# Two attention blocks on one core: four of a Strassen group's seven products add up in one PSUM bank

## The chip, the cores and the metric

The kernel runs on 1 core of one Trainium2 chip. The metric is device time in microseconds (us). Before the change it is 3025.81 us, the median of 3 runs (3024.51 to 3025.86). The engines are TensorE (PE; PEld is its weight load), VectorE (DVE), ScalarE (ACT), GpSimd (POOL) and SyncE (SP, which issues the DMAs).

## The reference, cut to what matters

x is 8 images of 512 channels by 1024 positions, in fp32. Two attention blocks follow each other, each with a residual.

```python
# block 0: group norm over 32 groups, 8 heads of 64 channels
h = group_norm(x, norm_w, norm_b)
q, k, v = split(qkv_w @ h + qkv_b)
attn = softmax(q^T k / sqrt(64))          # per head
x = x + proj_w @ (attn v) + proj_b
# block 1: norm over the whole image, one head of 512 channels
n = norm(x) * gn_gamma + gn_beta
q, k, v = wq @ n + bq, wk @ n + bk, wv @ n + bv
attn = softmax(q k^T * 512**-0.5)
x = x + wo @ (attn v) + bo
```

## The kernel before

The core works through the 8 images one after the other; everything is fp32, in tiles of 128 partitions by 512 columns. Weights of block 1 are multiplied together once (wq with wk, wv with wo), so that block 1 has a q, a v, scores and a weighted sum, and no k and no projection of its own.

All products of 512 channels by 1024 positions are split in quarters and done by Strassen's scheme in its Winograd form: 7 products of quarters instead of 8, with sums S1 to S4 of the one side's quarters (`finish`, L171) and T1 to T4 of the other's (`Combined`, L336). Output quarter (0,0) is P1+P2; U2 is P1+P6, U3 is U2+P7, U4 is U2+P5; then (0,1) is U4+P3, (1,0) is U3+P4 and (1,1) is U3+P5.

One group of seven products for a 128-by-512 piece of each output quarter is the generator `strassen` (L362). It is called with `multiply`, which puts a product into a PSUM bank (`by_channels` L422, `by_positions` L434 and local ones for the scores, L743, and the weighted sum, L805), and with `done`, which takes a finished output quarter to SBUF (L452, L466, L683, L750, L811). A product is two matmuls of 512 columns, or four of 256, and four matmuls in the weighted sum; in the profile each fp32 matmul is two rows. A group yields five times, and what the caller hangs on those steps (`at_steps`, hooks) is put between the steps: norms of the next image, sums T, loads.

PSUM is one pool with two tags, o and s, of two buffers each (`banks`, L90). A tile has two banks. A group before the change takes four of them: o for P1 and P2, s for P5 and P6, o for P7 and P4, s (or o) for P3. ACT copies P1 to SBUF as u1; VectorE makes u2, u4 and u3 with `plus` (L373), reading one bank and one SBUF tile each, and the four `done` passes. The u tiles come from a pool of five buffers (L83).

Engine orders of PE, ACT and DVE are those of the program text (`manual_schedule`, L836); a tile framework adds semaphores between engines. The order of an image is: v of block 0 (2 groups), q and k of chunks 1 and 3 of the four channel chunks (2), attention of 8 heads (no Strassen), the projection (2 groups in turn, `together`, L404, with the last divide as a hook, L694), q and k of chunks 0 and 2 for the next image (2, with block 1's norm in hooks, L868), q of block 1 (2), v (2), scores (4), and the weighted sum, called values here (2 groups in turn, with the sums S and T by `finish_values`, L781, in hooks 1, 3 and 5, and the next image's load, norm and T in `at_values`, L883). That is 18 groups per image, 4 of them in pairs that take turns. Hook n runs after step n of the stage. `sums` (L797) is called by the first `done` of the values stage and puts two reciprocals on VectorE.

The lines named by the steps of the prediction are: L427 and L441 (matmuls of q, k, p and of v), L745 (scores), L807 (values), L380 (ACT's copy u1), L375 (`plus`), L454, L468, L752, L817 (first passes of `done`), L326 and L328 (the two halves of a norm, ACT and DVE), L529 and L534 (`held` on ACT and the reciprocal on DVE), L793 (T of the values stage).

Of the kernel before, what the change touches and what calls it, by code (L numbers as in the profile page):

```python
# [59 lines left out]
def two_attention_blocks(  # L60
# [212 lines left out]
    class Norm:  # L273
# [45 lines left out]

        def normed(self, hs):  # L320
            for half in range(2):
                for cc in range(NC):
                    h, x = piece(hs, cc, half), piece(self.xs, cc, half)
                    scale, shift = self.scale[:, cc : cc + 1], self.shift[:, cc : cc + 1]
                    if cc % 2:
                        nc.scalar.activation(h, x, AF.Identity, bias=shift, scale=scale)  # L326
                    else:
                        nc.vector.tensor_scalar(h, x, scale, shift, ALU.mult, ALU.add)  # L328
# [32 lines left out]

    def strassen(multiply, done, name, last="s"):  # L362

        def two(tag, n, *parts):
            o = banks(tag, f"ps_{name}_{n}")
            for i, (a, b) in enumerate(parts):
                multiply(o[:, i, :], a, b)  # L370
            return o[:, 0, :], o[:, 1, :]

        def plus(bank, u, what):  # L373
            t = tile_u(f"{what}_{name}")
            nc.vector.tensor_tensor(t, bank, u, ALU.add)  # L375
            return t

        p1, p2 = two("o", 0, ("A11", "B11"), ("A12", "B21"))
        u1 = tile_u(f"u1_{name}")
        nc.scalar.copy(u1, p1)  # L380
        done(0, 0, p2, u1)
        yield
        o = banks("s", f"ps_{name}_1")
        p5, p6 = o[:, 0, :], o[:, 1, :]
        multiply(p5, "S1", "T1")
        yield
        multiply(p6, "S2", "T2")
        u2 = plus(p6, u1, "u2")
        u4 = plus(p5, u2, "u4")
        yield  # L390
        p7, p4 = two("o", 2, ("S3", "T3"), ("A22", "T4"))
        u3 = plus(p7, u2, "u3")
        done(1, 1, p5, u3)
        done(1, 0, p4, u3)
        yield
        p3, _ = two(last, 3, ("S4", "B22"))
        done(0, 1, p3, u4)
        yield
# [23 lines left out]
    def by_channels(w, c, bs):  # L422


        def multiply(bank, a, b):
            for k in range(2):
                nc.tensor.matmul(  # L427
                    bank, w[a][:, k, c * P : (c + 1) * P], bs[b][:, k, :],
                    start=k == 0, stop=k == 1,
                )  # L430

        return multiply

    def by_positions(w, n2, bs):  # L434


        def multiply(bank, a, b):
            for u in range(2):
                n = 2 * n2 + u
                for k in range(2):  # L440
                    nc.tensor.matmul(  # L441
                        bank[:, u * 2 * P : (u + 1) * 2 * P], bs[b][:, k, n * P : (n + 1) * P],
                        w[a][:, k, :], start=k == 0, stop=k == 1,
                    )

        return multiply

    def make_channels(w, c, oc, bs, bias, to, name, last="s"):

        def done(i, half, bank, u):  # L452
            n = oc + 2 * i
            nc.vector.scalar_tensor_tensor(  # L454
                to(n, half), bank, bias[:, n : n + 1], u, ALU.add, ALU.add
            )

        return strassen(by_channels(w, c, bs), done, f"{name}_{oc}", last)

    def make_v(w, n2, bs, vs, name):  # L460


        def pairs(t):
            return t.rearrange("p (u o) -> p u o", u=2)

        def done(i, half, bank, u):  # L466
            v = vs[2 * half + n2][:, :, i * 2 * P : (i + 1) * 2 * P]
            nc.vector.tensor_tensor(v, pairs(bank), pairs(u), ALU.add)  # L468

        return strassen(by_positions(w, n2, bs), done, f"{name}_{n2}")  # L470
# [72 lines left out]
    def pairs_qk(w, oc, bs, qs, ks, b):  # L543

        for ts, n, bias, name, last in [(qs, 0, V_BQ0, "q", "s"), (ks, 1, V_BK0, "k", "o" if oc else "s")]:
            for i in (oc, oc + 2):
                ts[i] = tile2(f"{name}_0_{b}_{i}")
            yield make_channels(
                w.parts[n], 0, oc, bs, vec[:, bias : bias + NC],
                lambda chunk, half, ts=ts: ts[chunk][:, half, :], f"{name}_0_{b}", last,  # L550
            )
# [3 lines left out]
    def layer0(bs, qs, ks, b, load_next, norm_next):  # L555
# [81 lines left out]
        if norm_next is not None:  # L637
            hooks[0] = [lambda: norm_next().mean_of_all()]
            hooks[2] = [lambda: norm_next().variance_of_all()]
            combine = Combined(f"0_{b + 1}")  # L640
            hooks[3] = [lambda: norm_next().normed(norm_next().xs)]
            hooks[5] = [lambda: combine.first(norm_next().xs)]
# [39 lines left out]
        def project(w, c):  # L682
            def done(i, half, bank, u):  # L683
                chunk = c + 2 * i
                t, x = tile_u(f"p_{b}_{chunk}_{half}"), piece(xs, chunk, half)
                nc.vector.scalar_tensor_tensor(  # L686
                    t, bank, bias[:, chunk : chunk + 1], u, ALU.add, ALU.add
                )
                nc.vector.tensor_tensor(x, x, t, ALU.add)  # L689
                norm.of_half(chunk, half)  # L690
# [15 lines left out]
    def attention1(xs, bs, b, at_values):  # L706
# [35 lines left out]
        def scores(t):  # L742
            def multiply(bank, a, b):  # L743
                for k in range(2):
                    nc.tensor.matmul(  # L745
                        bank, bs[b][:, k, t * P : (t + 1) * P], q_parts[a][:, k, :],
                        start=k == 0, stop=k == 1,
                    )

            def done(i, j, bank, u):  # L750
                p = ps[j][t // 2][i][:, t % 2, :]
                nc.vector.tensor_tensor(p, bank, u, ALU.add)  # L752
                nc.scalar.activation(p, p, AF.Exp, scale=C**-0.5)  # L753
                if late:
# [49 lines left out]
        def values(c):  # L804
            def multiply(bank, a, b):  # L805
                for kt in range(NT // 2):
                    nc.tensor.matmul(  # L807
                        bank, v_parts[kt // 2][a][:, kt % 2, c * P : (c + 1) * P],
                        p_parts[kt // 2][b][:, kt % 2, :], start=kt == 0, stop=kt == NT // 2 - 1,
                    )  # L810

            def done(i, j, bank, u):
                if not invs:
                    sums()
                chunk = c + 2 * i
                t, x = tile_u(f"o_1_{b}_{chunk}_{j}"), piece(xs, chunk, j)
                nc.vector.tensor_tensor(t, bank, u, ALU.add)  # L817
                nc.vector.tensor_tensor(t, t, invs[j], ALU.mult)  # L818
                nc.vector.scalar_tensor_tensor(  # L819
# [16 lines left out]
    with tc.manual_schedule(engines={PE, ACT, DVE}):  # L836
# [15 lines left out]
        for b in range(B):  # L852
            ahead = []

            def load_next():
# [7 lines left out]
            steps = [  # L863
                norm.mean_of_all, norm.variance_of_all, lambda: norm.normed(hs),
                lambda: combine.first(hs), combine.second,
            ]
# [9 lines left out]
            if b + 1 < B:  # L876
# [3 lines left out]
                def load_again():  # L880
                    again.xs = load_x(b + 1, nc.sync)

                at_values = {  # L883
                    2: [load_again], 6: [lambda: again.normed(again.xs)],
                    8: [lambda: combine_next.first(again.xs)], 9: [combine_next.second],
                }
# [409 lines left out]
```

## Time and profile before

| what | value |
|---|---|
| median of 3 runs | 3025.81 us |
| the profiled execution's own time | 3028.86 us |
| its span, first to last instruction | 3027.1 us |
| mean granted TensorE clock | 0.993 |
| attention of block 0, one image (1243.6 to 1360.9 us) | 117.3 us |
| projection (1360.9 to 1388.0) | 27.1 us |
| q and k for the next image, norm beside (1388.0 to 1414.2) | 26.2 us |
| q, v of block 1 (1414.2 to 1462.4) | 48.2 us |
| scores of block 1 (1462.4 to 1510.5) | 48.1 us |
| values of block 1 (1510.5 to 1561.1) | 50.6 us |

The profile is of one execution. Its page gives busy time by engine, the chain of work that ended last, and the costliest groups of instructions. A line of a group reads: line, engine, operation, out<-in with shapes, count, busy time and mean, then the idle time before it and who ended that. In the timeline the first two numbers are start and duration in us, and an idle time with its releaser stands in brackets. Matmuls are pipelined: a row's record is longer than the distance to the next row. The stages in the table are windows of image 3, counted from 0.

### The profile page before, as it was taken

Reading aid. Unit: us, or ns where it says so; the run is one execution under the profiler, and the core shown is the slowest. Engines: PE = TensorE matmul, PEld = TensorE weight load, DVE = VectorE, ACT = ScalarE, POOL = GpSimd, SP = SyncE. Lnnn points to the kernel's source line nnn. Section 1 sums busy time; section 2 is a strip of 40 time slices with the busy share of each in tenths; the row PEclk is TensorE's granted clock in tenths of the full one; section 3 lists DMA queues with packets and bytes.
Section 4 is the critical chain, followed back from the end, with each engine's and each line's share of the span. In section 5 each row is a group of like instructions: output and inputs, shape, how many; then the busy total and the mean of one; then the engine's idle time right before and its main releaser. Section 6 shows DMA issues by size and latency. Waiting matters only on the chain.

```text
span 3027.1 us, 33513 instructions
## 1 busy us (share of the span) xinstructions
PE 2966.2 (98%) x14082; PEld 1379.1 (46%) x14082; DVE 2234.1 (74%) x2746; ACT 899.1 (30%) x1265; POOL 13.9 (0%) x26
## 2 busy tenths in 40 slices
PE   7999999999999999999999999999999999999898
PEld 4533545335453455434553345533545335453353
DVE  4588577884778858787587965889667895668857
ACT  0163122621136111461115501154011640216311
POOL 0000000000000000000000000000000000000000
PEclk9999999999999999999999999999999999999999
DMA  6300213001130112201121020310212102120000
GB/s 238 140 13 25 73 35 125 2 27 71 50 111 1 49 49 83 77 1 49 49 96 65 1 73 25 108 53 1 73 38 95 53 25 73 35 96 3 1 0 29
DMA packets 49935, 167.41 MB, mean 55 GB/s; under 512 B 3440, under 2 KB 9584, under 8 KB 43376
## 3 DMA queue, kind: packets, MB, share of 16 engines
q1 hardware_dynamic: 45824, 160.97, 15.0%
q10 hardware_dynamic: 3952, 4.22, 0.4%
q8 instruction: 112, 1.84, 0.2%
q14 instruction: 47, 0.39, 0.0%
HBM read 137.39 MB, written 27.79 MB: 55 GB/s over the span
## 4 chain that ended last, share of the span: by engine, by line
PE 93%; DVE 6%; issue 0%; ACT 0%; DMA 0%; POOL 0%; POOLq 0%; DVEq 0%
PE s L583 15%; PE ps_o L604 15%; PE ps_q L427 13%; PE ps_v L441 13%; PE ps_s L745 13%; PE ps_o L807 9%; PE ps_k L427 6%; PE ps_p L427 5%; PE ps_sum L618 2%; DVE inv L534 2%; DVE p L686 1%; PE ps_wvo L509 1%; DVE x L819 0%; DVE x L689 0%; DVE o L818 0%; PE ps_sum L800 0%
## 5 line engine op out<-in xcount | busy, mean ns | idle before, releaser
L520 ACT ACTIVATE p<-s 128x1024 f32<-128x1024 f32 x512 | 523.5, 1024 | 333.6 <-PE s L583 329.6
L583 PE MATMUL s<-q,k 64*64 64x512 f32 x4096 | 533.8, 593 | 0.0
L604 PE MATMUL ps_o<-p,v 64*64 64x512 f32 x4096 | 528.7, 589 | 0.0
L522 DVE TENSOR_TENSOR acc<-acc,p 128x1024 f32<-128x1024 f32 x384 | 469.6, 1223 | 76.9 <-ACT p L520 61.9
L534 DVE RECIPROCAL inv<-ps_sum 128x512 f32<-128x512 f32 x80 | 268.4, 3355 | 40.4 <-ACT held_sum L529 40.4
L583 PEld LDWEIGHTS s<-q,k 64*64 64x64 f32 x4096 | 149.6, 133 | 300.6 <-issue 227.8
L604 PEld LDWEIGHTS ps_o<-p,v 64*64 64x64 f32 x4096 | 156.6, 133 | 282.8 <-issue 270.4
L807 PE MATMUL ps_o<-t_p,s_v 128*128 128x512 f32 x384 | 169.7, 595 | 3.6 <-DVE t_p L793 3.6
L745 PE MATMUL ps_s<-s_q,t 128*128 128x512 f32 x384 | 170.0, 592 | 0.0
L753 ACT ACTIVATE p<-p 128x512 f32<-128x512 f32 x128 | 80.1, 630 | 253.0 <-DVE p L752 253.0
L375 DVE TENSOR_TENSOR u_s<-ps_s,u_s 128x512 f32<-128x512 f32 x96 | 66.4, 692 | 117.6 <-PE ps_s L745 116.5
L380 ACT COPY u_v<-ps_v 128x512 f32<-128x512 f32 x32 | 18.7, 585 | 433.4 <-PE ps_v L441 433.4
L380 ACT COPY u_q<-ps_q 128x512 f32<-128x512 f32 x32 | 18.7, 585 | 413.5 <-PE ps_q L427 413.5
L375 DVE TENSOR_TENSOR u_q<-ps_q,u_q 128x512 f32<-128x512 f32 x96 | 66.4, 691 | 96.8 <-PE ps_q L427 95.7
L752 DVE TENSOR_TENSOR p<-ps_s,u_s 128x512 f32<-128x512 f32 x128 | 86.6, 687 | 68.6 <-ACT u_s L380 67.6
L468 DVE TENSOR_TENSOR v<-ps_v,u_v 128x512 f32<-128x512 f32 x128 | 82.7, 683 | 62.8 <-ACT u_v L380 61.7
L807 PEld LDWEIGHTS ps_o<-t_p,s_v 128*128 128x128 f32 x384 | 71.6, 190 | 99.1 <-issue 82.0
L745 PE MATMUL ps_s<-q,h 128*128 128x512 f32 x256 | 115.1, 592 | 0.0
L745 PEld LDWEIGHTS ps_s<-s_q,t 128*128 128x128 f32 x384 | 73.0, 190 | 91.8 <-issue 88.0
L441 PE MATMUL ps_v<-w_wvo,t 128*128 128x256 f32 x512 | 113.1, 379 | 0.0
L427 PE MATMUL ps_q<-t,w_wqk 128*128 128x512 f32 x256 | 112.5, 592 | 0.0
L807 PE MATMUL ps_o<-p,v 128*128 128x512 f32 x256 | 112.5, 592 | 0.0
(179 smaller groups left out, 3862.1 us busy)
## 6 DMA issues: line engine op xcount, KB each, us to landing
x<-in_x SPq DMA_DIRECT2D x88, 512.0 KB, 7.9
w_qk<-stored_qk SPq DMA_DIRECT2D x14, 1792.0 KB, 7.4
out<-x SPq DMA_DIRECT2D x32, 512.0 KB, 2.8
w_wqk<-stored_wqk SPq DMA_DIRECT2D x8, 1792.0 KB, 7.4
w_wvo<-stored_wvo SPq DMA_DIRECT2D x8, 1792.0 KB, 7.5
w_v<-stored_v SPq DMA_DIRECT2D x7, 1792.0 KB, 7.4
w_p<-stored_p SPq DMA_DIRECT2D x7, 1792.0 KB, 7.1
stored_qk<-w_qk SPq DMA_DIRECT2D x2, 1792.0 KB, 7.3
```

What stands on the lines that cost most here:

```text
L375: nc.vector.tensor_tensor(t, bank, u, ALU.add)
L427: nc.tensor.matmul(bank, w[a][:, k, c * P : (c + 1) * P], bs[b][:, k, :], start=k == 0, stop=k == 1,)
L441: nc.tensor.matmul(bank[:, u * 2 * P : (u + 1) * 2 * P], bs[b][:, k, n * P : (n + 1) * P], w[a][:, k, :], start=k == 0, stop=k == 1,)
L468: nc.vector.tensor_tensor(v, pairs(bank), pairs(u), ALU.add)
L520: nc.scalar.activation(p, s, AF.Exp, scale=factor)
L522: nc.vector.tensor_tensor(acc, first, p, ALU.add)
L534: nc.vector.reciprocal(inv, ps)
L583: nc.tensor.matmul(s[cols, j, :], flat(ks[pair])[rows, k0 : k0 + HD], qs[pair][rows, g, :], start=True, stop=True,)
L604: nc.tensor.matmul(o[cols, half, :], vs[kt][rows, c0 : c0 + HD], p[rows, j, :], start=kt == 0, stop=kt == NT - 1,)
L745: nc.tensor.matmul(bank, bs[b][:, k, t * P : (t + 1) * P], q_parts[a][:, k, :], start=k == 0, stop=k == 1,)
L752: nc.vector.tensor_tensor(p, bank, u, ALU.add)
L807: nc.tensor.matmul(bank, v_parts[kt // 2][a][:, kt % 2, c * P : (c + 1) * P], p_parts[kt // 2][b][:, kt % 2, :], start=kt == 0, stop=kt == ...
```

## The change

`strassen` takes one tile of tag o for a whole group: its first bank is the "line", in which P1, P6, P5 and P3 add up, without a new start; its second bank is "single", which takes P2 and later P4. P7 has the first bank of a tile of tag s. ACT copies the line to SBUF after P1 (u1), after P6 (u2) and after P5 (u4); after P3 the line is the output quarter (0,1) itself, and `done` gets None for u. VectorE adds only u3 = P7 + u2. The products come in the order P1, P2, P6, P7, P5, P4, P3 in place of P1, P2, P5, P6, P7, P4, P3. `multiply` gets `fresh`, which sets start only for the first matmul in a bank; for the v groups only the first of the two column halves sets it. `done` with None is an ACT instruction for q, k, v and the exponential of the scores, and a shorter VectorE chain in the projection and the values. The norms are put into hooks by halves. The number of matmuls is the same.

```diff
-    def strassen(multiply, done, name, last="s"):
...
-        p1, p2 = two("o", 0, ("A11", "B11"), ("A12", "B21"))
-        u1 = tile_u(f"u1_{name}")
-        nc.scalar.copy(u1, p1)
-        done(0, 0, p2, u1)
+    def strassen(multiply, done, name):
+        def copied(bank, what):
+            u = tile_u(f"{what}_{name}")
+            nc.scalar.copy(u, bank)
+            return u
+
+        o = banks("o", f"ps_{name}_0")
+        line, single = o[:, 0, :], o[:, 1, :]
+        multiply(line, "A11", "B11", True)
+        u1 = copied(line, "u1")
+        multiply(single, "A12", "B21", True)
+        done(0, 0, single, u1)
         yield
-        o = banks("s", f"ps_{name}_1")
-        p5, p6 = o[:, 0, :], o[:, 1, :]
-        multiply(p5, "S1", "T1")
+        multiply(line, "S2", "T2", False)
+        u2 = copied(line, "u2")
         yield
-        multiply(p6, "S2", "T2")
-        u2 = plus(p6, u1, "u2")
-        u4 = plus(p5, u2, "u4")
+        p7 = banks("s", f"ps_{name}_1")[:, 0, :]
+        multiply(p7, "S3", "T3", True)
+        u3 = tile_u(f"u3_{name}")
+        nc.vector.tensor_tensor(u3, p7, u2, ALU.add)
         yield
-        p7, p4 = two("o", 2, ("S3", "T3"), ("A22", "T4"))
-        u3 = plus(p7, u2, "u3")
-        done(1, 1, p5, u3)
-        done(1, 0, p4, u3)
+        multiply(line, "S1", "T1", False)
+        u4 = copied(line, "u4")
+        done(1, 1, p7, u4)
+        multiply(single, "A22", "T4", True)
+        done(1, 0, single, u3)
         yield
-        p3, _ = two(last, 3, ("S4", "B22"))
-        done(0, 1, p3, u4)
+        multiply(line, "S4", "B22", False)
+        done(0, 1, line, None)
         yield
...
-        def multiply(bank, a, b):
+        def multiply(bank, a, b, fresh):
             for k in range(2):
                 nc.tensor.matmul(
                     bank, w[a][:, k, c * P : (c + 1) * P], bs[b][:, k, :],
-                    start=k == 0, stop=k == 1,
+                    start=fresh and k == 0, stop=k == 1, skip_group_check=True,
                 )
...
             n = oc + 2 * i
-            nc.vector.scalar_tensor_tensor(
-                to(n, half), bank, bias[:, n : n + 1], u, ALU.add, ALU.add
-            )
+            if u is None:
+                nc.scalar.activation(to(n, half), bank, AF.Identity, bias=bias[:, n : n + 1])
+            else:
+                nc.vector.scalar_tensor_tensor(
+                    to(n, half), bank, bias[:, n : n + 1], u, ALU.add, ALU.add
+                )
...
-            hooks[3] = [lambda: norm_next().normed(norm_next().xs)]
+            for half in range(2):
+                hooks[3 + half] = [lambda half=half: norm_next().normed(norm_next().xs, [half])]
...
-                t, x = tile_u(f"p_{b}_{chunk}_{half}"), piece(xs, chunk, half)
+                x = piece(xs, chunk, half)
+                if u is not None:
+                    nc.vector.tensor_tensor(u, bank, u, ALU.add)
+                    bank = u
                 nc.vector.scalar_tensor_tensor(
-                    t, bank, bias[:, chunk : chunk + 1], u, ALU.add, ALU.add
-                )
-                nc.vector.tensor_tensor(x, x, t, ALU.add)
+                    x, bank, bias[:, chunk : chunk + 1], x, ALU.add, ALU.add
+                )
                 norm.of_half(chunk, half)
...
                 p = ps[j][t // 2][i][:, t % 2, :]
-                nc.vector.tensor_tensor(p, bank, u, ALU.add)
-                nc.scalar.activation(p, p, AF.Exp, scale=C**-0.5)
+                if u is not None:
+                    nc.vector.tensor_tensor(p, bank, u, ALU.add)
+                    bank = p
+                nc.scalar.activation(p, bank, AF.Exp, scale=C**-0.5)
...
-                norm.mean_of_all, norm.variance_of_all, lambda: norm.normed(hs),
-                lambda: combine.first(hs), combine.second,
+                norm.mean_of_all, norm.variance_of_all, lambda: norm.normed(hs, [0]),
+                lambda: norm.normed(hs, [1]), lambda: combine.first(hs), combine.second,
...
-                    2: [load_again], 6: [lambda: again.normed(again.xs)],
-                    8: [lambda: combine_next.first(again.xs)], 9: [combine_next.second],
+                    2: [load_again], 5: [lambda: again.normed(again.xs, [0])],
+                    6: [lambda: again.normed(again.xs, [1])], 8: [lambda: combine_next.first(again.xs)], 9: [combine_next.second],
```

## The prediction

> **What bounds the kernel now.** I read the page first (busy shares, then the chain that ended last), then TensorE's own waits, then the timeline of one image (1193 to 1565 us), and last the granted clock.
>
> ```profile
> PE 2966.2 (98%) x14082; PEld 1379.1 (46%) x14082; DVE 2234.1 (74%) x2746; ACT 899.1 (30%) x1265; POOL 13.9 (0%) x26
> ...
> PE 93%; DVE 6%; issue 0%; ACT 0%; DMA 0%; POOL 0%; POOLq 0%; DVEq 0%
> ```
>
> TensorE is the bound: 2966.2 of 3027.1 us, and 93% of the chain. VectorE at 74% is not, so taking passes from it pays only where TensorE waits for it:
>
> ```profile
> PE ps_p L427 <- DVE p L686: 10.9, 8, 1.4
> PE ps_q L427 <- DVE q L454: 10.2, 7, 1.5
> PE ps_o L807 <- DVE t_p L793: 3.6, 8, 0.5
> ```
>
> Three short waits per image (total, times, longest). (A row's pitch end is where the next row could have begun; its record ends 0.16 later.) From pitch end to the next row's start they are 1.6, 1.7 and 1.0 us (the last with a second one behind it), so all that a faster VectorE can give is 8 x (1.6 + 1.0) + 7 x 1.7 = 33 us.
>
> What the change can cost is read from how a Strassen product hands over. In the timeline of the scores stage (start, duration):
>
> ```profile
> 1462.25 3.60 PE L745 MATMUL ps_s<-q,h 128*128 128x512 f32 x8
> 1465.68 5.31 PE L745 MATMUL ps_s<-s_q,t 128*128 128x512 f32 x12
> 1465.93 0.58 ACT L380 COPY u_s<-ps_s 128x512 f32<-128x512 f32 x1 [11.48 <-PE ps_s L745]
> 1466.55 0.69 DVE L752 TENSOR_TENSOR p<-ps_s,u_s 128x512 f32<-128x512 f32 x1 [3.21 <-ACT u_s L380]
> ...
> 1469.32 1.42 DVE L375 TENSOR_TENSOR u_s<-ps_s,u_s 128x512 f32<-128x512 f32 x2 [2.08 <-PE ps_s L745]
> ```
>
> Eight rows are P1 and P2, so a product is 4 rows and 1.717 us (a stage of 112 rows lasts 48.07), a group 12.02. The copy of P1 begins 0.25 us after P2's pitch ended at 1465.68, not after P1: it waits for the other bank of the same tile as well. VectorE begins 0.21 after P6's pitch end (1469.11). And in the values stage:
>
> ```profile
> 1519.10 0.60 ACT L529 ACTIVATE held_sum<-ps_sum 128x512 f32<-128x512 f32 x1 [1.13 <-PE ps_sum L800]
> ...
> 1519.82 3.36 DVE L534 RECIPROCAL inv<-ps_sum 128x512 f32<-128x512 f32 x1 [2.34 <-ACT held_sum L529]
> ...
> 1523.21 0.60 ACT L529 ACTIVATE held_sum<-ps_sum 128x512 f32<-128x512 f32 x1 [3.42 <-DVE inv L534]
> ```
>
> ACT's read of the second bank waits for DVE's read of the first, though neither needs the other. **Accesses to one PSUM tile stand in line as a whole tile**, not by bank. What a wait costs TensorE at its end:
>
> ```profile
> 1531.98 1.22 DVE L793 TENSOR_TENSOR t_p<-p,t_p 128x1024 f32<-128x1024 f32 x1
> ...
> 1533.25 0.30 PEld L807 LDWEIGHTS ps_o<-t_p,s_v 128*128 128x128 f32 x2 [1.28 <-DVE t_p L793]
> ...
> 1533.79 0.19 PEld L807 LDWEIGHTS ps_o<-t_p,s_v 128*128 128x128 f32 x1 [0.24 <-issue]
> ```
>
> VectorE ends at 1533.20, the weights start 0.05 later, and as the next load comes with the second row at 1533.79, the first row began at 1533.36: 0.16 us from release to pitch.
>
> **The change, part by part.** The number of matmuls stays. Per group VectorE loses three passes and ACT gains three; ACT is busy 30%. The order of products becomes P1, P2, P6, P7, P5, P4, P3. The tile of tag o now holds "line" (P1, P6, P5, P3) and "single" (P2, P4), and the built program lists TensorE waits by that whole tile: P2 waits for the copy of P1; P6 for the VectorE pass on P2; P5 for the copy of P6; P4 for the copy of P5; P3 for the pass on P4. Before, each of these had another tile. Only P5's wait has a product (P7, 1.72 us) beside it; the other four stand bare.
>
> *Plain groups* (q, k, v, scores; one group at a time): P2: 0.20 (the q copy at 1391.58, behind a pitch end of 1391.38, has one semaphore to wait for) + 0.58 + 0.16 = 0.94. P6: 0.26 (0.21 and 0.05 for a second semaphore, as 0.25 stands to 0.20) + 0.69 + 0.16 = 1.11. P4: 0.25 + 0.58 + 0.16 = 0.99. P3: 0.21 + 0.69 + 0.16 = 1.06. Sum 4.10; with the bias pass of 0.74 (L454) in place of 0.69, 4.20. Behind a waiting matmul all of TensorE stands; nothing else fills it. Groups: 48 for q and k, 32 for v, 32 for scores: 48 x 4.20 + 64 x 4.10 = **464 us**.
>
> *Project* (two groups a, b in turn, 27.06 us before with its stall). Partner products cover P6 and P3, not P2 and P4: 4 x 0.95. P6 moves ahead of P5, and needs T2, which comes out of the last divide: P2a ends at 4.4 us from the start, sum to 5.4, VectorE's done pass, reciprocal 3.36, product 0.69 and T2 0.69 to 11.3; P2b ends at 9.9: 1.6 lost, and 0.25 at P6b behind T3 and T4. With the old 1.6 gone I get 30.9: **+3.85 x 8 = 31**.
>
> *Values* (two groups, 3.43 us a product, 50.8 before). P2a stalls 0.94, and the sums end at 9.57 from the start. P2b waits for its copy, which stands on ACT behind the second held_sum, itself behind the first reciprocal: 15.36 in place of 13.0. P6a needs S2 and T2, two steps earlier than now: reciprocals end at 18.0, two done chains of 2.07 each follow to 22.1, S2 0.6 and T2 1.2: start 24.06, while P2b ended at 18.8. 5.3 us stand bare. P4a and P4b lose 0.99 each; the rest is covered. End 60.4: **+9.6 x 8 = 77**. The x loads issue behind the same chain as now (21.1 then, 22.1 after) and land some 5 us later (ACT's L326 at 1536.95), ahead of the halves of the norm at 31.
>
> *Norm halves*: the ACT half (2 x 0.735) stands ahead of one u1 copy in each of 14 stages and delays it 0.37: **+5**. Cover gone entirely, 1.5 x 14 = 21. *The q stall* of 1.7 goes, 7 times: **-12**; what is late there next is P3's bare wait, counted above.
>
> *The clock.* An idle TensorE can lose its clock:
>
> ```profile
> 42.00:45.00 3.00, 0.27 (x2) 0.11 (x2) 2.90 (x5) 0.58 (x1) 0.00 (x0) 1.00 1.09 459
> ...
> 104.00:108.00 4.00, 4.00 (x39) 4.00 (x38) 3.31 (x7) 0.58 (x1) 0.00 (x0) 1.00 0.00 0
> 108.00:112.00 4.00, 4.00 (x22) 4.00 (x22) 3.90 (x11) 0.00 (x0) 0.00 (x0) 0.54 0.96 401
> ```
>
> (Third last column: granted clock.) 2.7 us idle at 42 left it at 1.00; 9 us of one-column matmuls from 103.5 halved it, and the 8 rows of q behind took 6.60 instead of 3.60 us, 3.0 lost. The 5.3 us of the values stage lie between: 0 to 3.0, I take 1.3, **+10**. The Trainium skill ("TensorE: Matmul & The Clock Gate", section "What's actually happening") puts the loss of the clock at an idle window of about 3.4 us; by it the 5.3 us would lose it in most images and the 1.1 us waits never, an estimate of up to 8 x 2.
>
> Sum: 464 + 31 + 77 + 5 - 12 + 10 = +575. The profiled execution took 3028.86 (span 3027.1), 0.1% above the median 3025.81. 3028.9 + 575 = 3604, scaled to the runs 3600.
>
> **The rivals.**
> 1. *The waits go by bank.* Then line waits only for line: P2, P7 and P4 cover every copy, and no bare wait is left in a plain group. For it: ACT has 70% idle. Against: the copy at 1465.93 and the turn-taking of held_sum and reciprocal, and the program's waits. T2's earlier need stays: project +1.0, values 23.0 - 15.5 - 1.0 = +6.6, less 12: 8 x 7.6 - 12 = +49, 3078. The Trainium skill ("PSUM — Partial Sum Buffer", section "PSUM bank collisions raise a hardware error") asks for a guard only by bank and quadrant; by that rule the sum is 3078, by the rows 3600.
> 2. *Faster: the lighter VectorE wins.* Place: the three waits shown; price -33, 2996. It decides if the bare waits stay under 33 / 112 = 0.3 us a group, against 4.1. For it: 432 passes of 0.69 go. Against: each handover takes 0.9 us in the rows above.
> 3. *The stop-and-go halves the clock.* A plain group would then run at three quarters activity; at half clock all 112 would add 112 x 12 = 1340: up to 4940. Against: full clock at 42 to 48 with one third idle.
>
> **How the numbers follow.** My sum 0.86; waits by bank 0.06; half clock 0.05; lighter VectorE 0.02; a draw 0.01. 448 bare waits carry 464 us: 0.1 us on each is 45. Low end 3540: each wait 0.1 shorter, no clock loss. High end 3690: 0.15 more on each wait for queues on ACT and DVE (67) and 3.0 instead of 1.3 us of clock (14). The other cases lie outside and are left out. About 0.2% is what a measurement of this kernel can tell from no change: faster 0.02, same 0.01, slower 0.97.
>
> **What would show it.** In the profile after: TensorE's busy share falls from 98% to about 83%; its waits name ACT's copy (about 0.95 each) and VectorE's done pass for ps_q, ps_k, ps_v and ps_s; a plain group's pitch is 16.1 us and the scores stage 64; the values stage shows one wait near 5 us for t_p. Right in mechanism, wrong in size, if P6 or P3 shows other gaps than 1.1. Wrong altogether if the scores stage still takes 48 us.

## The result, and the profile after

The changed kernel takes 3603.47 us (median of 4 runs, 3601.66 to 3603.95) against 3025.68 us beside it (4 runs, 3024.51 to 3025.86): ratio 1.1909, 95% interval 1.1889 to 1.193. The forecast was 3600. The profiled execution has a span of 3602.2 us, 575 more than the 3027.1 of before, at a mean granted clock of 0.986 against 0.993.

Busy time by engine and, below it, the chain of work that ended last, both from the page of after:

```profile
PE 3127.6 (87%) x14082; PEld 1352.9 (38%) x14082; DVE 1964.8 (55%) x2314; ACT 1111.4 (31%) x1633; POOL 13.9 (0%) x26
...
PE 83%; DVE 9%; ACT 5%; issue 2%; DMA 0%; DVEq 0%; ACTq 0%; POOL 0%; POOLq 0%
```

VectorE lost 432 instructions and 269 us, and TensorE runs the same 14082 rows. Its busy share is 87% and not the 83% that the prediction named: the same rows show 161 us more of busy time, since four rows behind a wait have a record of 1.98 us in place of 1.88, and rows at half clock last longer. But TensorE is no longer busy throughout, and VectorE and ACT now hold 14% of the chain, where they held 6%: links of the chain that used to lie beside matmuls lie between them. TensorE's waits in after (engine, tile, line, releaser: total, times, longest):

```profile
PE ps_q L425 <- DVE q L457: 59.3, 64, 5.8
PE ps_s L754 <- DVE p L762: 52.4, 64, 0.9
PE ps_v L440 <- DVE v L474: 52.3, 64, 0.9
PE ps_s L754 <- ACT u_s L370: 44.9, 64, 0.7
PE ps_v L440 <- ACT u_v L370: 44.8, 64, 1.0
PE ps_q L425 <- ACT u_q L370: 44.7, 64, 1.0
PE ps_o L818 <- DVE t_p L804: 36.9, 8, 5.1
PE ps_o L818 <- ACT u_o L370: 31.6, 32, 1.9
```

q, v and the scores have 32 plain groups each, and each of the three shows 64 waits for the done pass and 64 for the copy: two of each per group, four in all. One plain group, in the timeline of the scores stage of after (start, duration; in brackets the idle time before and its releaser):

```profile
1750.73 1.88 PE L754 MATMUL ps_s<-q,h 128*128 128x512 f32 x4
...
1752.65 0.58 ACT L370 COPY u_s<-ps_s 128x512 f32<-128x512 f32 x1 [1.12 <-PE ps_s L754]
...
1753.28 1.98 PE L754 MATMUL ps_s<-q,h 128*128 128x512 f32 x4 [0.68 <-ACT u_s L370]
...
1755.38 0.69 DVE L762 TENSOR_TENSOR p<-ps_s,u_s 128x512 f32<-128x512 f32 x1 [5.13 <-PE ps_s L754]
...
1756.12 5.42 PE L754 MATMUL ps_s<-s_q,t 128*128 128x512 f32 x12 [0.85 <-DVE p L762]
...
1758.20 0.58 ACT L370 COPY u_s<-ps_s 128x512 f32<-128x512 f32 x1 [1.47 <-PE ps_s L754]
...
1762.27 1.98 PE L754 MATMUL ps_s<-q,t 128*128 128x512 f32 x4 [0.73 <-ACT u_s L370]
...
1765.04 1.99 PE L754 MATMUL ps_s<-s_q,h 128*128 128x512 f32 x4 [0.79 <-DVE p L762]
...
1766.86 1.45 PE L754 MATMUL ps_s<-q,h 128*128 128x512 f32 x3
```

P2 starts after the copy of P1, P6 after the pass on P2, P4 after the copy behind P5, P3 after the pass on P4. The twelve rows at 1756.12 are P6, P7 and P5 without a gap: the copy of P6 at 1758.20 ends under P7, and so P5 is the one that doesn't wait. The idle times in brackets (0.68, 0.85, 0.73, 0.79) are shorter than the loss, because a record ends later than the place where the next row could have begun. The pitch tells the whole of it: P1 of this group begins at 1750.73, P1 of the next at 1766.86 (last line, cut off by the end of the window), 16.13 us in place of 12.02. With 1.717 us for a product, P2, P6, P4, P3 and the next P1 start 0.83, 1.12, 1.00, 1.05 and 0.10 us late, 4.10 together; the 0.10 of a P1 that waits for nothing suggests that a row behind a wait is recorded 0.1 early, which puts P2's own share at 0.93.

The stages, from first row to first row, summed over the eight images (us):

| stage | before | after | difference |
|---|---|---|---|
| scores (32 groups) | 384.5 | 516.1 | +131.6 |
| v of block 0 | 193.4 | 258.8 | +65.4 |
| v of block 1 | 193.4 | 259.4 | +66.0 |
| q of block 1 | 195.0 | 263.9 | +68.9 |
| q of block 0 | 217.4 | 277.7 | +60.3 |
| k of block 0 | 194.6 | 257.1 | +62.5 |
| projection (8 pairs) | 227.3 | 254.1 | +26.8 |
| values (8 pairs) | 408.1 | 502.4 | +94.3 |
| attention of block 0 | 947.0 | 947.0 | 0 |

The values stage of image 3, three lines of TensorE, and below it the stage in stretches of 4 us (the third number from the right is the granted clock):

```profile
1808.64 3.60 PE L818 MATMUL ps_o<-p,v 128*128 128x512 f32 x8
1814.17 5.40 PE L818 MATMUL ps_o<-p,v 128*128 128x512 f32 x8 [1.93 <-ACT u_o L370]
1823.67 8.53 PE L818 MATMUL ps_o<-t_p,s_v 128*128 128x512 f32 x13 [4.10 <-DVE t_p L804]
```

```profile
1811.10:1815.10 4.00, 2.07 (x5) 0.68 (x4) 3.25 (x2) 1.16 (x3) 0.00 (x0) 1.00 0.00 0
1815.10:1819.10 4.00, 4.00 (x7) 1.54 (x5) 3.92 (x4) 0.00 (x0) 0.00 (x0) 0.57 0.00 0
1819.10:1823.10 4.00, 0.46 (x2) 0.00 (x0) 3.36 (x5) 0.00 (x0) 0.00 (x0) 0.90 0.08 29
1823.10:1827.10 4.00, 3.43 (x4) 1.51 (x5) 4.00 (x6) 0.00 (x0) 0.00 (x0) 0.50 1.01 320
```

The first row is P1b. The second is P2b: it waits for its copy, which stands on ACT behind held_sum, and then runs its eight rows in 5.40 us instead of some 3.7, at a clock of 0.57. The third is P6a, which waits for T2 and runs at half clock.

### The profile page after: what moved, and what is told of

Same layout as the page of the kernel before. It is cut to its first block, busy times and chain, and to the rows that moved or that the text cites. A ratio compares the mean times of both kernels' runs of the same rounds, so it can differ in the third digit from the quotient of the medians.

```text
span 3602.2 us, 34028 instructions
## 1 busy us (share of the span) xinstructions
PE 3127.6 (87%) x14082; PEld 1352.9 (38%) x14082; DVE 1964.8 (55%) x2314; ACT 1111.4 (31%) x1633; POOL 13.9 (0%) x26
## 4 chain that ended last, share of the span: by engine, by line
PE 83%; DVE 9%; ACT 5%; issue 2%; DMA 0%; DVEq 0%; ACTq 0%; POOL 0%; POOLq 0%
PE s L589 13%; PE ps_o L610 12%; PE ps_q L425 12%; PE ps_v L440 12%; PE ps_s L754 12%; PE ps_o L818 10%; PE ps_k L425 5%; PE ps_p L425 4%; DVE inv L540 2%; PE ps_sum L624 2%; DVE q L457 1%; DVE p L762 1%; DVE v L474 1%; ACT u_v L370 1%; ACT u_s L370 1%
## 5 line engine op out<-in xcount | busy, mean ns | idle before, releaser
L818 PE MATMUL ps_o<-t_p,s_v 128*128 128x512 f32 x384 | 184.2, 640 | 36.9 <-DVE t_p L804 36.9
L762 DVE TENSOR_TENSOR p<-ps_s,u_s 128x512 f32<-128x512 f32 x96 | 66.4, 692 | 256.2 <-PE ps_s L754 204.2
L474 DVE TENSOR_TENSOR v<-ps_v,u_v 128x512 f32<-128x512 f32 x96 | 66.4, 692 | 239.8 <-PE ps_v L440 201.4
L370 ACT COPY u_v<-ps_v 128x512 f32<-128x512 f32 x96 | 56.2, 585 | 355.9 <-PE ps_v L440 355.9
L370 ACT COPY u_q<-ps_q 128x512 f32<-128x512 f32 x96 | 56.2, 585 | 351.9 <-PE ps_q L425 351.9
L754 PE MATMUL ps_s<-q,h 128*128 128x512 f32 x256 | 123.7, 606 | 21.6 <-ACT u_s L370 21.6
L818 PE MATMUL ps_o<-p,v 128*128 128x512 f32 x256 | 123.5, 628 | 20.8 <-ACT u_o L370 20.8
L425 PE MATMUL ps_p<-t_p,w_p 128*128 128x512 f32 x256 | 119.7, 606 | 21.3 <-ACT u_p L370 10.8
L440 PE MATMUL ps_v<-w_v,t_again 128*128 128x256 f32 x448 | 104.2, 386 | 21.8 <-DVE v L474 11.9
L425 PE MATMUL ps_q<-x,w_qk 128*128 128x512 f32 x192 | 99.1, 641 | 26.3 <-DVE q L457 12.7
```

Source lines behind the costliest of these rows:

```text
L370: nc.scalar.copy(u, bank)
L425: nc.tensor.matmul(bank, w[a][:, k, c * P : (c + 1) * P], bs[b][:, k, :], start=fresh and k == 0, stop=k == 1, skip_group_check=True,)
L440: nc.tensor.matmul(bank[:, u * 2 * P : (u + 1) * 2 * P], bs[b][:, k, n * P : (n + 1) * P], w[a][:, k, :], start=fresh and u == k == 0, sto ...
L754: nc.tensor.matmul(bank, bs[b][:, k, t * P : (t + 1) * P], q_parts[a][:, k, :], start=fresh and k == 0, stop=k == 1, skip_group_check=True,)
L818: nc.tensor.matmul(bank, v_parts[kt // 2][a][:, kt % 2, c * P : (c + 1) * P], p_parts[kt // 2][b][:, kt % 2, :], start=fresh and kt == 0, ...
```

## The experiments

The theory of the prediction: accesses to one PSUM tile stand in line as a whole tile, so that four handovers of a plain group stand bare; beside it S2 and T2 of the values stage are due two steps earlier. The main rival: the waits aren't for the tile, and the cost lies elsewhere (in the new order of the products, in ACT, in the clock). Times in us; each time is read beside runs of the kernel before on the same chip, whose medians were 3026.05, 3027.31 and 3025.59. A time without a range is that of one execution. Cuts in code and profile are marked by dots; of each edit the lines that matter are shown. The expectations call the kernels by short names: pairs_old is the kernel of the second experiment, apart_pairs_old that of the first.

### The line in a tile of its own

The order of the products, the copies on ACT and the adding up in one bank all stay; P2 and P4 only move out of the line's tile. The two paired stages have their old scheme here, as in the next experiment, so that the two kernels differ only in these tiles.

```diff
-        line, single = o[:, 0, :], o[:, 1, :]
+        line = o[:, 0, :]
...
+        single = banks("s", f"ps_{name}_2")[:, 0, :]
         multiply(single, "A12", "B21", True)
...
+        single = banks("s", f"ps_{name}_4")[:, 0, :]
         multiply(single, "A22", "T4", True)
```

> As pairs_old, but in the groups of q, k, v and scores P2 and P4 get tiles of tag s of their own, so that line is alone in its tile; order of products, ACT copies and VectorE passes stay as changed. Theory (the whole-tile order is what costs): P2, P7 and P4 cover the copies, a plain group is 12.02 us again, the 1.7 us stall ahead of k is gone 7 times: 3025.7 - 12 = 3014, between 3005 and 3022. Rival (the chain copy to next product on the line costs, or the three added ACT passes): each group keeps at least its waits of P6, P5 and P3, 2 to 3 us a group, 3250 to 3400.

Measured, 8 runs: 3035.31 (3033.76 to 3037.27), ratio 1.0029 (1.0018 to 1.0039); the kernel of the next experiment, with line and single in one tile, takes 3525.87. The scores stage is back at 48.07 us, q of block 1 at 24.03, v of block 1 at 24.17. One group of the scores:

```profile
1465.97 3.60 PE L788 MATMUL ps_s<-q,h 128*128 128x512 f32 x8
...
1467.89 0.58 ACT L370 COPY u_s<-ps_s 128x512 f32<-128x512 f32 x1 [1.13 <-PE ps_s L788]
1469.40 5.31 PE L788 MATMUL ps_s<-s_q,t 128*128 128x512 f32 x12
...
1474.55 1.88 PE L788 MATMUL ps_s<-q,t 128*128 128x512 f32 x4
...
1476.27 1.88 PE L788 MATMUL ps_s<-s_q,h 128*128 128x512 f32 x4
...
1477.99 2.31 PE L788 MATMUL ps_s<-q,h 128*128 128x512 f32 x5
```

The copy of P1 begins 0.20 us after P1's pitch end (1467.69), under P2; in the kernel before it began after P2. No row of the group waits, and the next group begins after 12.02 us. The four bare waits have left the list of TensorE's waits; its head is now:

```profile
PE ps_p L461 <- DVE p L729: 10.9, 8, 1.4
PE ps_wvo L551 <- DMA wo<-in_w_o: 10.0, 1, 10.0
PE ps_v L476 <- DVE t_again L353: 6.4, 7, 0.9
```

So the theory holds against the rival: with the same products, the same order and the same copies, the whole-tile wait alone makes the plain groups' loss. It is a wait that the program sets: in after TensorE's wait ends with a semaphore of ACT or VectorE, for a read of the other bank, and it is gone when the two banks lie in two tiles. The Trainium skill ("PSUM — Partial Sum Buffer", section "PSUM bank collisions raise a hardware error") asks for a guard by bank and quadrant only, and the 12.02 agrees with it; the program before this edit waited for more. The size was missed by 21 us (3014 was expected). The stages show where: v of block 0 takes 25.35 instead of 24.17, since P7 now comes earlier and waits for T3 (the third line above); the second k group 10.81 instead of 10.39 in seven images; the very first q group 19.7 instead of 16.6. Against that, q behind the projection takes 13.25 instead of 14.08, half of the 1.7 us that were expected there.

### The old pairs

The projection and the values go back to the scheme of before, with their done chains; the plain groups stay changed.

```diff
-            return strassen(by_channels(w, c, comb), done, f"p_0_{b}_{c}")
+            return strassen_old(by_channels(w, c, comb), done, f"p_0_{b}_{c}")
...
-            return strassen(multiply, done, f"o_1_{b}_{c}")
+            return strassen_old(multiply, done, f"o_1_{b}_{c}")
```

> The projection and the values stage go back to the scheme of before (four tiles a group, P5 ahead of P6, seven VectorE passes); q, k, v and scores keep the changed scheme. Theory (bare waits on one shared PSUM tile, the same in every group, additive over stages): the stage lengths of the two profiles differ by 26.8 us in the projection and by 94.3 in the values, so 3603.5 - 121 = 3482 us, and the scores stage stays at 64.5. Rival (the clock: the changed values stage with its long idle throws the clock of the stages behind it, so that more comes back than its own share): below 3460.

Measured: 3525.87, 44 more than expected. The two stages did as expected (projection 27.05, values 50.62, scores unchanged at 64.52). The 44 us came up behind them: the v pair of block 0 rose from 32.4 to as much as 37.8, the q group behind the projection from 16.4 to 17.9 and 19.6. The timeline at that border, first TensorE, then VectorE:

```profile
1390.38 1.99 PE L474 MATMUL ps_v<-w_v,x 128*128 128x256 f32 x8 [0.68 <-ACT u_v L370]
1395.80 7.13 PE L474 MATMUL ps_v<-w_v,t_again 128*128 128x256 f32 x24 [3.43 <-DVE v L508]
```

```profile
1390.68 0.68 DVE L862 TENSOR_TENSOR o<-ps_o,u_o 128x512 f32<-128x512 f32 x1
1391.40 0.69 DVE L863 TENSOR_TENSOR o<-o,inv 128x512 f32<-128x512 f32 x1
1392.13 0.75 DVE L864 SCALAR_TENSOR_TENSOR x<-o,bias,x 128x512 f32<-128x512 f32 x1
1392.80 1.22 DVE L353 TENSOR_TENSOR t_again<-x,x 128x1024 f32<-128x1024 f32 x1
1393.93 1.22 DVE L354 TENSOR_TENSOR t_again<-x,t_again 128x1024 f32<-128x1024 f32 x1
1395.07 0.68 DVE L508 TENSOR_TENSOR v<-ps_v,u_v 128x512 f32<-128x512 f32 x1
```

When P2 of the first v group starts (1390.38), VectorE still has five instructions of the values stage and of the sums T ahead of it. The pass on P2 (last line) stands behind them, and P6 waits for that pass: 3.43 instead of 0.85. The clock falls as well: the 24 rows behind take 7.13 instead of the 5.45 us of the next group. Together 2.58 + 1.68 = 4.26, and the pair takes 36.6 instead of 32.4. Before the change the same backlog was there and met no wait, because P5 stood in another tile. This reading was put to the test:

```diff
-            in_turn(*[make_v(w, n2, bs, vs, f"v_0_{b}") for n2 in range(2)]), hooks)
+            in_turn(*[make_v(w, n2, bs, vs, f"v_0_{b}", strassen_old if n2 == 0 else None) for n2 in range(2)]), hooks)
...
+                strassen_old if oc == 0 and name == "q" else None,
```

> The kernel with the old pairs once more (3525.9), with two plain groups of each image put back to the old scheme as well: the first v group behind the values stage and the first q group behind the projection. It asks whether the 44 us that the old pairs cost beyond the sum sit at those two borders. Backlog at the border (VectorE still has the sums and done chains of the pair to do when the next group begins, and only P6's bare wait on the done pass of P2 makes TensorE wait for it): the v pair of block 0 falls from 32.4 to 37.8 us to 12.1 + 16.2 = 28.3 in every image (289.4 to 226 over all), the q group behind the projection from 17.9 to 19.6 to before's 14.1 (157.3 to 115.2 over eight), the very first second q group from 21.9 to some 16; time 3525.9 - 63 - 42 - 5 = 3416. Rival, the backlog is handed on to the second group, whose waits are still bare: only the bare waits of the 16 groups go, 16 x 4.1 = 66, and the time stays at or above 3451.

Measured: 3422.39, 6 more than expected. The v pairs of block 0 take 28.23 in every image (225.8 in all, without the making of weights that stands inside the first), the q group behind the projection 14.08. The backlog isn't handed on; it costs only where a bare wait meets it. (The very first second q group took 20.15, not the 16 expected, a miss of 4.)

### S2 and T2 of the values stage made early

```diff
         finish_values(1)
-        hooks = {1: [lambda: finish_values(2)], 3: [lambda: finish_values(3)], 5: [lambda: finish_values(4)]}
+        finish_values(2)
+        hooks = {3: [lambda: finish_values(3)], 5: [lambda: finish_values(4)]}
```

> The changed kernel, with S2 and T2 of the values stage computed ahead of the stage, with S1 and T1, in place of behind its second step. Theory (P6 stands for T2, which stands behind two reciprocals and two done chains, and the idle drops the clock): the 4 to 5 us wait for t_p goes, and with it 1.6 to 2.8 us of slow rows behind: 8 x (4.5 + 2.2) = 54, so 3549; with the clock unaffected 3567. Rival (P6 would wait anyway for the done pass that stands behind the same reciprocals): 3600.

Measured: 3547.3. The values stage falls from 502.4 to 445.9 in all, and no other stage moves by more than 1.5 us. So 56 of the 94 us of this stage are P6a's wait for T2 and the clock behind it. The forty rows from P6a on take 17.36 without a wait ahead of them.

### Matmuls in the gap ahead of P6a

Four matmuls of 512 columns are put ahead of P6a; nothing reads what they write. The wait stays as long as it was, but TensorE is kept active in it.

```diff
+        def fill():
+            t = banks("s", f"ps_fill_1_{b}")
+            for i in range(4):
+                nc.tensor.matmul(t[:, i % 2, :], ones, acc[:, i % 2, :], start=True, stop=True)
+
-        hooks = {1: [lambda: finish_values(2)], 3: [lambda: finish_values(3)], 5: [lambda: finish_values(4)]}
+        hooks = {1: [lambda: finish_values(2), fill], 3: [lambda: finish_values(3)], 5: [lambda: finish_values(4)]}
```

> The changed kernel, with 4 extra matmuls of 512 columns ahead of P6 of the values stage (their output is read by nobody), so that TensorE works 3.4 of the 4 to 5 us in which it stood for T2. Theory (that idle drops the clock, and the slow rows behind cost 1.6 to 2.8 us): granted clock 1.00 behind the wait, the values stage 60 to 61 us in place of 61.7 to 63.6, total 3603 - 8 x 2 = 3587. Rival (the rows behind are slow for another reason): no gain, 3603 or above.

Measured: 3585.87, with 64 matmul rows more than after. The values stage falls to 488.0 in all, 60.9 in six images and 60.22 in one; the last is named below. In the image of the next lines the fill covers the gap but for 0.67 us, and P6a's forty rows take 17.45, as in all eight images, where after's take 18.90 to 20.12:

```profile
1807.04 5.40 PE L818 MATMUL ps_o<-p,v 128*128 128x512 f32 x8 [1.93 <-ACT u_o L370]
1812.28 3.60 PE L847 MATMUL ps_fill<-acc,ones 128*128 128x512 f32 x8
1816.54 17.45 PE L818 MATMUL ps_o<-t_p,s_v 128*128 128x512 f32 x40 [0.67 <-DVE t_p L804]
```

```profile
1806.00:1810.00 4.00, 2.96 (x4) 1.31 (x5) 3.45 (x2) 0.99 (x3) 0.00 (x0) 0.69 0.00 0
1810.00:1814.00 4.00, 4.00 (x10) 1.68 (x9) 3.28 (x6) 0.00 (x0) 0.00 (x0) 0.88 0.01 2
1814.00:1818.00 4.00, 3.33 (x9) 1.24 (x7) 4.00 (x5) 0.00 (x0) 0.00 (x0) 1.00 0.58 173
```

The clock ahead of P6a is 1.00. P2b still lost it in the gap of 1.93 before (5.40). The image of 60.22 is one in which P2b kept it too: this is the stage without any loss of clock. The last image, whose stage ends otherwise, kept it at both places as well and took 62.37.

### One copy twice, a bare one and a covered one

In the scores stage the copy behind P5 (u4), whose end P4 waits for, is issued a second time; in another kernel the copy behind P6 (u2), which P7 covers.

```diff
         u4 = copied(line, "u4")
+        if name.startswith("s_1"):
+            nc.scalar.copy(u4, line)
```

```diff
         u2 = copied(line, "u2")
+        if name.startswith("s_1"):
+            nc.scalar.copy(u2, line)
```

> The changed kernel, with the copy u4 of the scores groups issued twice on ACT (same output). Theory (P4 stands bare behind that copy): the second copy of 0.5 to 0.6 us lengthens each of 32 groups by as much, scores stage 64.5 + 2.2 = 66.7, total + 17 = 3621. Rival (ACT at 31% busy hides its copies, the wait ends by something else): no change, 64.5 and 3603.

> The changed kernel, with the copy u2 of the scores groups issued twice on ACT. Theory (only u2 has a product beside it: 0.25 + 0.58 + 0.48 + 0.16 = 1.47 of the 1.72 us of P7): scores stage still 64.5, total 3603. Rival (every longer copy is paid, cover or not): 67.0 as with u4.

Measured: u4 3614.36, the scores stage 66.99 instead of 64.51 in each image, 2.48 / 4 = 0.62 a group, a whole copy (0.58) and a little more; u2 3602.08, the scores stage 64.29. With u4 twice P4's wait is 1.35 where it was 0.73:

```profile
1747.70 1.98 PE L756 MATMUL ps_s<-q,t 128*128 128x512 f32 x4 [1.35 <-ACT u_s L391]
```

The same instruction on the same engine costs all of its time in one place and nothing in the other. The u4 kernel as a whole rose by 11 and not by the 17 expected: the scores stages cost 19.8 more, but the values stages fell from 502.4 to 497.8, where P2b kept its clock in seven of eight images, and the kernel up to the end of its first q groups is some 4.5 us shorter. ACT's load as such (31%) is no cause.

### Only the order: P6 ahead of P5

In the kernel before, P5 and P6 change places; everything else, the tiles too, is as before.

```diff
-        multiply(p5, "S1", "T1")
+        multiply(p6, "S2", "T2")
         yield
-        multiply(p6, "S2", "T2")
+        multiply(p5, "S1", "T1")
```

> The kernel before, whose only edit is the order: P6 one step ahead of P5, in the same tile, everything else as it was. Theory (the order of products alone costs in the pairs, as T2 comes behind the divide and behind the reciprocals): one wait of 7 to 8 us a values stage for t_p in place of 1.0, one of 2.6 in the projection, and slow rows behind the long one: 3026 + 8 x (6.6 + 1.0) + 8 x (2 to 3) = 3103 to 3111, plain groups at 12.02. Rival (T2 is there in time, the order is free): 3026.

Measured: 3131.55, some 20 more than the upper end of what was expected. Plain groups stay at 12.02 (scores 48.07). The values stage takes 59.2 to 60.4 in place of 50.62, the projection 31.06 in place of 27.05 in six images (29.36 in the first):

```profile
PE ps_o L807 <- DVE t_p L793: 58.6, 8, 7.3
PE ps_p L427 <- DVE t_p L662: 17.0, 8, 2.1
PE ps_p L427 <- DVE p L686: 10.8, 8, 1.4
```

The early need of T2 is shown apart from the tiles. The projection's wait for T2 (2.1) comes on top of its old one (1.4, as before). The clock falls at both places, to 0.56 behind the 7.3 us (1572 to 1576) and to 0.63 behind the 2.1 us (1411 to 1415). The stage lengths show where the 20 us more lie. The values stages cost 75 in all, inside the 69 to 77 of the expectation; the projections cost 29 and not 8: their old wait stays, which the expectation took for gone, and the clock falls, which it had not priced there.

### Better versions, and whose gain it is

The kernel with the line in its own tile and the old pairs, with S2 and T2 early, and with the old scheme in the first v group behind the values stage and in the very first q group:

```diff
+        finish_values(2)
-        hooks = {1: [lambda: finish_values(2)], 3: [lambda: finish_values(3)], 5: [lambda: finish_values(4)]}
+        hooks = {3: [lambda: finish_values(3)], 5: [lambda: finish_values(4)]}
...
+            in_turn(*[make_v(w, n2, bs, vs, f"v_0_{b}", strassen_old if n2 == 0 else None) for n2 in range(2)]), hooks)
...
+                strassen_old if (b, oc) == (0, 0) and name == "q" else None,
```

> apart_pairs_old with two more edits: S2 and T2 of the values stage ahead of the stage, and the scheme of before for the first v group of block 0 and for the first q group of the kernel, the two places where P7 or P6 stood for T3 or T2 of a late VectorE. Theory (what apart_pairs_old lost to before is just these places: 8.3 us at v, 3 at the start; and the values stage has 1.0 to give): 3035 - 8 - 3 - 8 = 3016, 0.3% faster than before. Rival (VectorE's backlog only moves on and meets the next group): 3026 to 3035.

Measured, 9 runs: 3019.4 (3015.97 to 3021.31), ratio 0.9975 (0.9965 to 0.9985): 0.25% faster than the kernel before, by an interval that leaves out 1. By stages against before: values -6.0, q of block 0 -6.4, k +2.9. The next kernel takes from it only what owes nothing to the change, the early S2 and T2, and puts them into the kernel before:

```diff
         finish_values(1)
-        hooks = {1: [lambda: finish_values(2)], 3: [lambda: finish_values(3)], 5: [lambda: finish_values(4)]}
+        finish_values(2)
+        hooks = {3: [lambda: finish_values(3)], 5: [lambda: finish_values(4)]}
```

> The kernel before, with the sums S2 and T2 of the values stage made ahead of the stage; nothing of the change is in it. It asks what of the better version's gain (3019.4 against 3027.3) is owed to the change at all. Theory: the values stage falls from 50.62 to 49.88 us as it did there, all else stays: -6, 3021. Rival, the line in its own tile is what helps: no difference from before, 3027.

Measured, 10 runs: 3021.04, ratio 0.9982 (0.9973 to 0.9992); values 49.88 in every image but the last (52.96). So 4.6 us of gain, against 7.9 of the better version, come from this edit, which works in the old scheme as well. The two intervals overlap; that any of the rest is owed to the change is not shown. The third is the better version with `strassen_old`, the old scheme as it is written out in these kernels, for the k groups too:

```diff
-                strassen_old if (b, oc) == (0, 0) and name == "q" else None,
+                strassen_old if name == "k" or (b, oc, name) == (0, 0, "q") else None,
```

> The better version (line alone in its tile, S2 and T2 of values early, old scheme where a group follows a pair) with the old scheme for the k groups too. By the stages: the second k groups go from 10.81 back to 10.39, -3 in all, the rest stays, 3016.5. Rival: k's old P5 and P6 take the s tiles that the next q group needs, q goes from 13.25 back to 14.07, +6, 3022.

Measured, 10 runs: 3020.33, ratio 0.9985 (0.9975 to 0.9994): no gain over the better version. k went back to 10.39 and q kept its 13.25, as expected, but a new wait stands at the seam of k and attention:

```profile
PE ps_k L461 <- DVE k L493: 7.2, 8, 1.0
```

P3 of the second k group, which runs behind the first rows of attention, waits some 0.95 us for a k pass in seven images, and from those rows to P3 it is 2.04 us in place of 1.02 (1.64 in the last image). Neither the expectation nor its rival had that. A difference in the code stands beside it: `strassen_old` puts P3 into a tile of tag s always, while the kernel before gives this one group's P3 a tile of tag o (`last`, L545), and there P3 has no such wait. So this run is not the old scheme for these groups to the letter; that the tag alone makes the wait was not tested.

## Why the prediction was right, point by point

**The plain groups** were priced at 464, with +5 for the norm halves and -12 for the q stall, 457 in all; the six plain rows of the table add up to 454.7. The group's pitch was priced at 12.02 + 4.10 = 16.12 and is 16.13. Twice u4 shows that what is added to a bare handover is paid in full; the line in its own tile shows the cause. Where the sum was too high is k: the second k group pays 3.38 and not 4.20 (10.39 + 1.92 to 13.78 + 1.91), 6.6 us in all. Attention rows already stand ahead of its last four rows, and so P3's wait has a cover there. Where it was too low is the start: the first two q groups of the kernel pay 9.2 and 6.5 us (16.6 to 25.8 and 15.5 to 22.0). The first has the longest q wait of the list, 5.8 us for a done pass, the second runs at half clock for 12.9 us in place of 5.9. The prediction priced neither, and that this nearly cancels against k is luck.

**The projection** was priced at +3.85 an image and is +3.92 (27.05 to 30.97) in seven images; the last, whose stage ends otherwise, pays nothing (37.93 to 37.33). Sum 26.8 instead of 31. The terms as they stand in the prediction (4 x 0.95, 1.6 and 0.25, less 1.6) add up to 4.05 and not 3.85.

**The values stage** was priced at +9.6 an image for its waits. The image of 60.22 without any loss of clock gives 60.22 - 50.62 = +9.6, the last image 62.37 - 53.70 = +8.7: 76 in all for the 77 of the forecast.

**The clock** is the term that was mis-sized. The prediction took 10 us in all, 1.3 an image, for the 5.3 us of P6a alone. Measured: the first seven images of after last 437.7 together, 16.1 more than 7 x 60.22, and the last 64.72, 2.3 more than 62.37; 18 in all, 2.3 an image. Two things were missed. P6a loses its clock in every image: forty rows in 18.90 to 20.12 instead of 17.36. And P2b's gap of 1.93 us, where I had looked for no loss, costs P2b its clock in four of eight images. The +8 here, the -4 in the projection and the -2 in the plain groups nearly cancel, so that the sum of 575 is met so closely is luck; that the mechanism and the main terms are met is not.

**Rival 1**, waits by bank, fell as a forecast for this kernel and stands as a mechanism: with the line apart a plain group takes 12.02 again. Its price for the early T2 alone (8 x 7.6 = 61, without the -12) was too low: P6 ahead of P5 cost 104, with the clock in it. **Rival 2**, the lighter VectorE, fell: 269 us less work there, and TensorE's short waits for it were worth 33 at most. **Rival 3**, the half clock, fell in the plain groups: their four rows of a product take 1.98 us with a bare wait ahead of them, a group keeps its pitch of 16.1, and the six stages together cost 454.7, not 1340 more.

What the prediction said nothing of is that its terms depend on each other. It added the pairs and the plain groups up as if each could be taken back alone; taking the pairs back brought 78 us instead of the 121 expected, since the waits of one stage had hidden VectorE's backlog from the next.

In which images P2b loses its clock, the traces' record of the granted clock shows. In each run every change of the clock falls on a grid of 3.41 us, to within 0.01 us. Five kernels have the gap ahead of P2b (after, S2 and T2 early, the fill, each copy twice), 40 gaps in all, 2.09 us long from pitch end to the next row. In all 17 cases in which the gap begins between 0.11 us before and 1.14 us after a point of the grid, the clock falls; in none of the 23 in which it begins 1.27 to 3.19 us after one. In after it falls in images 2, 3, 5 and 7, which begin 0.65, 0.03, 0.64 and 1.14 after one, and is kept in the others, at 1.27 and at 3.12 to 3.15. So the phase decides. In all 17 at least 1.98 us of the gap lie in one stretch between two points of the grid; in four of the 23 they do too, but there the gap begins late, at 1.27 to 1.40 us, and reaches to the stretch's end. The Trainium skill ("TensorE: Matmul & The Clock Gate", section "What's actually happening") says the clock is judged over windows of some 3.4 us that run freely, and the grid agrees with it; but it names an idle window of about 3.4 us as what loses the clock, and here 2 us of idle time within one stretch were enough, as measured. In the scores stage of after no stretch has more than 1.6 us of idle time, and the clock is kept throughout. Where between 1.6 and 2 us the limit lies, why a late gap is spared, and what sets a run's phase, stays open.

## What to carry to other kernels

Before putting two accumulators into one PSUM tile, look in the trace whether a reader of one bank holds up a writer of the other; if so, price each handover as handover + operation + restart (here 0.9 to 1.1 us for an operation of 0.6 to 0.7), and count only those with no independent matmul between them. Work taken from an engine that isn't the bound is worth what the bound waits for it, here 33 us at most against 269 us of work. And a wait has no price of its own: an engine's backlog that cost nothing becomes TensorE's idle time as soon as the first wait of the next stage asks for that engine.

## What the runs showed of the hardware that was not expected

A gap of 1.93 us between TensorE's records was enough, in 17 of 40 cases and by its place on a grid of 3.41 us, to bring the granted clock from 1.00 to 0.50 for one stretch of that grid and eight rows from 3.70 to 5.40 us; gaps of 0.7 to 0.9 us, four to a group of 16 us, left the scores stage within 0.02 us of 64.51 in every image. Matmuls whose result nobody reads kept the clock: with 3.4 us of them in the gap the forty rows behind took 17.45 instead of 18.90 to 20.12 us, and the one execution of that kernel was 18 us faster than after with more work in it.
